# A GNN, mixer and FFN layer: the mixer's products on quarters of the array, its columns laid out so that neighbours are summed, three elementwise steps rewritten, and the FFN weight transposes moved last

## The chip, the cores and the metric

One Trainium2 chip, one of its cores. The time is the device time of one execution in microseconds (us), the median over several runs. The profile is one further execution, recorded by the hardware profiler. The engines are TensorE (PE, with its weight loads shown apart as PEld), VectorE (DVE), ScalarE (ACT), GpSimd (POOL) and SyncE (SP, which here only issues DMAs). Each engine works through its own list of instructions in the order in which they were compiled, and waits at an instruction whose inputs are not there.

## The reference

`x` has 1250 rows of 1024. There are 20000 edges with a source, a destination and one of 8 types.

```python
xn = layernorm(x)
# 1. GNN: per type r the mean over incoming edges, times weight[r]; gate z
u = xn @ root + bias + sum_r mean_r(xn[src]) @ weight[r]
z = concat([u, xn]) @ w_gate + b_gate
gnn = tanh(u) * z + xn * (1 - z)
# 2. mixer: linear attention, 8 heads of 16, features 1, k, k (x) k / sqrt(2)
q, k, v = rms_norm(xn) @ (w_q, w_kv)          # 128 columns each
num = phi(q) @ (phi(k).T @ v);  den = phi(q) @ sum(phi(k))
mix = (num / max(den, 1e-5)) @ w_out
x1 = x + gnn + mix
# 3. FFN with weights and inputs rounded to a 4-bit grid in blocks of 16
h = silu(Q(ln(x1)) @ Q(f_gate).T) * (Q(ln(x1)) @ Q(f_up).T)
out = x1 + Q(h) @ Q(f_down).T                  # 352 hidden columns
```

## The kernel before

Rows are handled in 10 blocks `b` of 128 (the last has 98). The kernel has four stages.

1. Up to about 350 us of the profiled execution: layer norm and transpose of all blocks, the edges sorted by destination, the first products `xn @ weight[r]`.
2. Up to about 1513 us: `product` multiplies `xn` by the other weights, in three products of parts per product (lines 520 to 522). Beside it run the *messages* for each half `nh` of the columns: `gather` (line 435, POOL) fetches 128 rows of `y_d` by an indirect DMA, and `segments` scales them (lines 446 and 448), sums equal destinations by two products with a selection matrix (lines 451 and 452), and stores the sums to `seg_d` (lines 453 and 454). There are 157 messages per half; four buffers `msg` hold gathered rows.
3. The list `rest`, up to about 1687 us. Its pieces are closures that are called in a written order. The loop over them issues, between the pieces, the last messages of the second half, so many per piece that the last one falls before the last `FIRST` = 5 pieces. The order of each engine's instructions is then settled by the compiler's scheduler, near this order.
4. `block(b)`, `hidden`, `finish`: for each block the gate product, the sum `x1`, its layer norm, rounding, and the FFN, software-pipelined over three blocks.

The pieces of stage 3 before the change, in the order of `rest`: four FFN transposes `gate_up` (`ffn_weight`: load a rounded weight tile into `raw`, transpose it on PE, copy it to `wguT`); `mix_sums` (lines 669 and 675); `open_rows` and `open_segments(0)` (segments that cross a tile border: sums of rows of `seg_d` are added to other rows of `seg_d` by indirect DMAs, line 757); four `mix_pair(c)`; eight more `gate_up`; eight `down` (the same transposes, into `wdT`); five `mix_num(b)`. When the last message has been issued, `open_segments(1)` follows. It loads rows of `seg_d` (lines 748 and 749, on SP's queue), multiplies, copies to `osum` and adds to `seg_d`. Only after that may `block` gather its rows `ag` (line 802).

`mix_pair(c)` forms, for two heads and each block, `kk[p, h, i, e] = k[p, h, i] * v[p, h, e]` on DVE (line 686, 512 columns), and a product sums it over the rows with all 128 columns of `k` as the stationary side (line 688). Of the 128 rows of the result only the 32 of the two heads are wanted: line 690 masks the rest to zero when it copies into `bd[:, c, :]`. There are 10 x 4 of these products.

`mix_num(b)` transposes `q` (line 622), and for each of four `c` multiplies it by `bd[:, c, :]` (line 629, 128 rows of contraction of which 96 are zero), multiplies the result by `q` along `i` (`prod`, line 631) and sums over `i` (`num`, line 633). In `prod` the index `i` lies outside `e`, so that the sum runs over elements 16 apart. A further product (lines 635 and 636) gives the linear and constant terms, seven small DVE steps follow (lines 637 to 645), and `mix_transposed` (lines 652 and 653) puts the result into `mixT`. Five of the ten `mix_num` are in `rest`; number 5 comes before the first block and 6 to 9 between later blocks.

In `block(b)` `xn` is made anew from `x` on DVE (line 124), `u` is the sum of the root product and `ag` (line 808), its transpose goes to PE (line 154), ACT takes the tanh (line 811), POOL forms `tanh(u) - xn` and `xn + x` (lines 812 and 813). PE then multiplies by `wg` (line 817) and `wo` (line 820); DVE adds and multiplies (lines 818 to 824). The second normalisation (line 124 again) and `quantize` (lines 133 to 146) are on DVE. `hidden` transposes the result and multiplies by `wguT` (line 841), `finish` by `wdT` (line 857).

Products of stage 3 and 4 write to a pool of four PSUM banks (`mm_tile`), transposes to one of two (`tr_tile`). The pool `wk` of stage 4 lies in memory that the pools of stage 3 gave up, so its first writers wait for the last use of these.

Of the kernel before, what the change touches and what calls it, by code (L numbers as in the profile page):

```python
# [8 lines left out]
F32 = mybir.dt.float32  # L9
# [3 lines left out]
AF = mybir.ActivationFunctionType  # L13
# [12 lines left out]
MORE = 4096  # L26
H, DH = 8, 16
FIRST = 5
LAG = 2
EARLY = 140  # L30
PLAIN = 4
# [11 lines left out]
def rows_of(b):  # L43
    return min(BR, N - b * BR)
# [3 lines left out]
def gps_layer(ctx: ExitStack, tc: tile.TileContext, x, src, dst, et, w_rel, w_root, bias,  # L48
# [24 lines left out]
    def mm_tile():  # L73
        return psum["mm"].tile([128, 512], F32, name="mm")
# [33 lines left out]

    stat = const.tile([BR, NB, 2], F32, name="stat")
    rms = const.tile([BR, NB, 2], F32, name="rms")  # L110
    V.memset(rms, 1.0)
    node_at = const.tile([128, NHI], I32, name="node_at")

# [9 lines left out]
    def normalize(o, xt, mr):  # L123
        V.tensor_scalar(o, xt, mr[:, 0:1], mr[:, 1:2], op0=ALU.subtract, op1=ALU.mult)  # L124
# [488 lines left out]
    bd = mx.tile([128, 4, 512], F32, name="bd")  # L613
# [5 lines left out]
    def mix_num(b):  # L619
        pt = tr_tile()  # L620
        n = rows_of(b)
        T.transpose(pt[:, 0, :n], qn[:n, b, :], ident[:n, :n])
        qT = mx.tile([128, BR], F32, name="qT", bufs=2)[:, :n]
        S.copy(qT, pt[:, 0, :n])
        q3 = h3(qn[:n, b, :])
        num = mx.tile([BR, H, DH], F32, name="num", bufs=2)[:n]
        for c in range(4):
            ps = mm_tile()
            T.matmul(ps[:n], qT, bd[:, c, :], start=True, stop=True)  # L629
            prod = mx.tile([BR, 2, DH, DH], F32, name="prod", bufs=2)[:n]  # L630
            V.tensor_tensor(prod, ps[:n].rearrange("p (h i e) -> p h i e", h=2, i=DH),  # L631
                            q3[:, 2 * c:2 * c + 2, :, None].to_broadcast([n, 2, DH, DH]), ALU.mult)
            V.tensor_reduce(num[:, 2 * c:2 * c + 2], prod.rearrange("p h i e -> p h e i"), AX.X, ALU.add)  # L633
# [12 lines left out]
        nums[b] = num  # L646
# [7 lines left out]

    with ExitStack() as late:
        op = late.enter_context(tc.tile_pool(name="op", bufs=1))
        pb = late.enter_context(tc.tile_pool(name="pb", bufs=2))
        kv = op.tile([BR, NB, 257], F32, name="kv")
        V.memset(kv[:, :, 256:257], 1.0)

# [15 lines left out]
            V.tensor_copy(crow[:, :128], ps[:1, :128])  # L676
            V.memset(crow[:, 128:], float(N))

        def mix_pair(c):
            ps = mm_tile()  # L680
            for b in range(NB):
                n = rows_of(b)
                kk = pb.tile([BR, 2, DH, DH], F32, name="kk")[:n]
                ck = kv[:n, b, c * 32:c * 32 + 32].rearrange("p (h i) -> p h i", h=2)
                cv = kv[:n, b, 128 + c * 32:128 + c * 32 + 32].rearrange("p (h e) -> p h e", h=2)
                V.tensor_tensor(kk, ck[:, :, :, None].to_broadcast([n, 2, DH, DH]),
                                cv[:, :, None, :].to_broadcast([n, 2, DH, DH]), ALU.mult)
                T.matmul(ps, kv[:n, b, :128], kk.rearrange("p h i e -> p (h i e)"),
                         start=(b == 0), stop=(b == NB - 1))
            V.scalar_tensor_tensor(  # L690
                bd[:, c, :].rearrange("p (h x) -> p h x", h=2), ps.rearrange("p (h x) -> p h x", h=2), 0.5,
                mask8[:, 2 * c:2 * c + 2][:, :, None].to_broadcast([128, 2, 256]), op0=ALU.mult, op1=ALU.mult)

# [50 lines left out]
        def open_segments(nh):  # L744
            s1 = op.tile([128, HD], F32, name="s1")
            s2 = op.tile([128, HD], F32, name="s2")
            rows127 = seg_d[nh][:ZERO, :].rearrange("(t p) c -> t p c", p=128)[:, 127, :]
            nc.sync.dma_start(s1, rows127[:128])
            nc.sync.dma_start(s2[:B2], rows127[128:])
            for i, n in enumerate((128, B2)):  # L750
                ps = mm_tile()
                T.matmul(ps[:n], osel[:, 0, i * 128:i * 128 + n], s1, start=True, stop=(i == 0))
                if i == 1:
                    T.matmul(ps[:n], osel[:B2, 1, 128:], s2[:B2], start=False, stop=True)
                osum = op.tile([128, HD], F32, name="osum", bufs=2)
                evac(osum[:n], ps[:n])
                G.indirect_dma_start(
                    out=seg_d[nh][:, :], out_offset=bass.IndirectOffsetOnAxis(ap=orow[:n, i:i + 1], axis=0),
                    in_=osum[:n, :], in_offset=None, compute_op=ALU.add)
# [6 lines left out]
        gate_up = [lambda a=(fgu_d[i * I:(i + 1) * I, :], r0, n, c0, HD, wguT, D_CHUNKS[:4], i * I + r0): ffn_weight(*a)  # L766
                   for i in range(2) for r0, n in I_CHUNKS for c0 in (0, HD)]
        down = [lambda a=(fdn_d, r0, n, 0, I, wdT, I_CHUNKS, r0): ffn_weight(*a) for r0, n in D_CHUNKS]
        rest = gate_up[:4] + [mix_sums, open_rows, lambda: open_segments(0)]
        rest += [lambda c=c: mix_pair(c) for c in range(4)] + gate_up[4:] + down  # L770
        for b in range(FIRST):
            rest.append(lambda b=b: (mix_num(b), mix_transposed(b - 1) if b else None))
        done = EARLY
        for i, p in enumerate(rest):
            p()
            while done < ST + LAG and (done - EARLY) * (len(rest) - FIRST) < (i + 1) * (ST + LAG - EARLY):
                message(1, done)
                done += 1
                if done == ST + LAG:
                    open_segments(1)  # L780
# [6 lines left out]

    turn[0], turns[0] = 1, 0
    wk = ctx.enter_context(tc.tile_pool(name="wk", bufs=1))
    def block(b):  # L790

        rows, n = block_rows(b), rows_of(b)
        xt = ld.tile([BR, D], F32, name="xt")[:n]
        rt = ld.tile([BR, D], F32, name="rt")[:n]
        ag = wk.tile([BR, D], F32, name="ag", bufs=2)[:n]
        gx = ld.tile([BR, D], F32, name="gx")[:n]
        nc.sync.dma_start(xt, x[rows, :])
        nc.sync.dma_start(rt, root_d[rows, :])
        nc.sync.dma_start(gx, gx_d[rows, :])
        with tc.issue_after(gathered_last[0]):  # L800
            for nh, cs in halves:
                G.indirect_dma_start(
                    out=ag[:, cs], out_offset=None, in_=seg_d[nh][:, :],
                    in_offset=bass.IndirectOffsetOnAxis(ap=node_at[:n, b:b + 1], axis=0))
        xn = wk.tile([BR, D], F32, name="xn", bufs=2)[:n]
        normalize(xn, xt, stat[:n, b, :])
        u = wk.tile([BR, D], F32, name="u", bufs=2)[:n]
        V.tensor_tensor(u, rt, ag, ALU.add)
        uT = wk.tile([128, KC, BR], F32, name="uT", bufs=2)
        transpose_cols(uT, u, n, D_CHUNKS, 0)  # L810
        S.activation(u, u, AF.Tanh)
        G.tensor_tensor(u, u, xn, ALU.subtract)
        G.tensor_tensor(xn, xn, xt, ALU.add)
        for nh, cs in halves:
            ps = mm_tile()
            for k in range(KC):
                T.matmul(ps[:n], uT[:, k, :n], wg[:, k, cs], start=(k == 0), stop=(k == KC - 1))  # L817
# [3 lines left out]
            V.tensor_tensor(xn[:, cs], pm[:n], xn[:, cs], ALU.add)  # L821
        V.tensor_tensor(gx, gx, u, ALU.mult)
        x1 = wk.tile([BR, D], F32, name="x1", bufs=3)[:n]
        V.tensor_tensor(x1, xn, gx, ALU.add)

        mr = wk.tile([BR, 2], F32, name="mr", bufs=2)[:n]
        mean_rstd(wk, mr, x1)
# [72 lines left out]
```

## Time and profile before

| | us |
|---|---|
| median of 3 runs | 2048.61 |
| lowest and highest run | 2047.39, 2053.55 |
| the profiled execution, whole | 2055.06 |
| its span from the first to the last instruction | 2053.3 |
| busy in the span: PE, PEld | 1932.2, 1282.5 |
| DVE, ACT, POOL | 1371.5, 719.9, 611.6 |

The span is what the profile's views divide; 1.8 us of the execution lie around it. Busy time of PE counts a product from its start to its modelled end, and products overlap, so that it says little on how well PE is used. In the profile an fp32 product or transpose appears as two records: 40 products of line 629 are 80 records of MATMUL.

### The profile page before, as it was taken

To read this page: it belongs to the slowest core of one execution; us is meant where nothing else is said; L and a number is where in the kernel's file an instruction comes from. 1 tells how busy PE (TensorE), PEld (TensorE's weight loads), DVE (VectorE), ACT (ScalarE), POOL (GpSimd) and SP (SyncE) were. 2 spreads that over 40 slices of the span, in tenths; PEclk is the share of its full clock that TensorE was granted. 3 is DMA by queue.
4 is the path that set the end of the run, shared out by engine and by line. 5 is a ranking of instruction groups with operands and counts; after the bars stand their busy time and mean duration, and the time that the engine had idled before them with its cause. 6 is when DMAs were issued, how large, how long until landed. Compare 5 with 4: busy or idle time off the path is not lost. (4 is left out here: it accounts for less than half of the span.)

```text
span 2053.3 us, 23776 instructions
## 1 busy us (share of the span) xinstructions
PE 1932.2 (94%) x7748; PEld 1282.5 (62%) x7748; DVE 1371.5 (67%) x2944; ACT 719.9 (35%) x1265; POOL 611.6 (30%) x539
## 2 busy tenths in 40 slices
PE   7999999999999999999999989989988879999998
PEld 4465544777777777777777866766753334455544
DVE  8989941677766456545554676665655767988785
ACT  4111241111125545455445455555542211222221
POOL 1000287885013323233323233323332122221110
PEclk9999999999999999999999999999987979999999
DMA  5233222444347776777766688778797422122100
GB/s 205 70 109 123 81 68 63 118 124 125 122 138 234 226 233 215 219 229 229 227 202 220 204 258 255 239 231 255 236 306 259 125 63 82 51 75 75 47 21 29
DMA packets 159346, 327.81 MB, mean 160 GB/s; under 512 B 26414, under 2 KB 35284, under 8 KB 159222
## 3 DMA queue, kind: packets, MB, share of 16 engines
q10 hardware_dynamic: 76570, 141.23, 18.6%
q0 software_dynamic: 33952, 91.27, 17.3%
q1 hardware_dynamic: 48700, 93.79, 14.5%
q8 instruction: 61, 1.00, 0.2%
q14 instruction: 63, 0.52, 0.1%
HBM read 179.54 MB, written 146.49 MB: 159 GB/s over the span
## 5 line engine op out<-in xcount | busy, mean ns | idle before, releaser
L520 PE MATMUL ab<-wH,xH 128*128 128x512 f32 (+3 forms) x1360 | 536.2, 395 | 3.4 <-ACT wH L479 3.2
L522 PE MATMUL ab<-wD,xD 128*128 128x512 f32 (+3 forms) x1360 | 529.9, 395 | 5.8 <-DVE wD L481 4.6
L521 PE MATMUL ab<-wL,xL 128*128 128x512 f32 (+3 forms) x1360 | 532.8, 393 | 0.0
L435 POOL DMA_INDIRECT msg<-y_d,key x314 | 319.5, 1018 | 677.3 <-PE sm L452 388.1
L448 DVE SCALAR_TENSOR_TENSOR msg<-msg,weight,hi 128x512 fp32r<-128x512 f32 x314 | 234.2, 750 | 148.6 <-ACT hi L446 95.1
L522 PEld LDWEIGHTS ab<-wD,xD 128*128 128x128 f32 (+1 forms) x1360 | 253.2, 187 | 77.0 <-DVE wD L481 13.6
L520 PEld LDWEIGHTS ab<-wH,xH 128*128 128x128 f32 (+1 forms) x1360 | 255.3, 188 | 62.1 <-ACT wH L479 5.4
L379 PE MATMUL mm<-wt,xnT 128*128 128x512 f32 (+1 forms) x640 | 292.1, 601 | 0.0
L521 PEld LDWEIGHTS ab<-wL,xL 128*128 128x128 f32 (+1 forms) x1360 | 254.4, 187 | 60.3 <-DVE wL L480 1.1
L361 POOL DMA_INDIRECT sort_d<-pay,row x160 | 202.1, 1263 | 281.7 <-DVE pay L352 233.3
L453 ACT COPY seg<-sm 128x512 f32<-128x512 f32 x314 | 181.6, 584 | 208.4 <-PE sm L452 153.2
L446 ACT ACTIVATE hi<-msg,weight 128x512 fp32r<-128x512 f32 x314 | 221.6, 721 | 89.8 <-DMA msg<-y_d,key 29.7
L529 DVE SCALAR_TENSOR_TENSOR yt<-ab,yt 128x512 f32<-128x512 f32 (+3 forms) x170 | 114.8, 680 | 120.8 <-ACT yt L528 117.0
L528 ACT ACTIVATE yt<-ab 128x512 f32<-128x512 f32 (+3 forms) x170 | 100.0, 592 | 269.2 <-PE ab L521 207.4
L379 PEld LDWEIGHTS mm<-wt,xnT 128*128 128x128 f32 (+1 forms) x640 | 114.6, 188 | 119.7 <-issue 118.7
L444 DVE TENSOR_SCALAR sel<-iota_n,last_row 128x128 fp32r<-128x128 f32 x314 | 89.8, 288 | 111.3 <-PE sm L452 108.5
L451 PE MATMUL sm<-hi,sel 128*128 128x512 f32 x314 | 138.3, 444 | 26.6 <-ACT hi L446 20.6
L452 PE MATMUL sm<-msg,sel 128*128 128x512 f32 x314 | 139.5, 444 | 24.5 <-DVE msg L448 24.3
L817 PE MATMUL mm<-wg,uT 128*128 128x512 f32 (+1 forms) x320 | 141.2, 594 | 1.2 <-ACT uT L87 0.8
L480 DVE TENSOR_TENSOR wL<-raw,h 128x512 fp32r<-128x512 f32 x136 | 93.0, 684 | 69.9 <-PE mm L379 69.9
L479 ACT CAST wH<-h 128x512 fp32r<-128x512 f32 x136 | 83.6, 621 | 132.6 <-DVE h L478 113.5
L817 PEld LDWEIGHTS mm<-wg,uT 128*128 128x128 f32 (+1 forms) x320 | 59.2, 187 | 75.1 <-issue 70.3
(257 smaller groups left out, 2153.9 us busy)
## 6 DMA issues: line engine op xcount, KB each, us to landing
seg_d<-seg ACTq DMA_DIRECT2D x314, 256.0 KB
y_d<-yt ACTq DMA_DIRECT2D x144, 256.0 KB
raw<-in_L_gnn_weight_dram SPq DMA_DIRECT2D x96, 256.0 KB
db<-in_dst_dram SPq DMA_DIRECT2D x32, 312.5 KB
xt<-in_x_dram SPq DMA_DIRECT2D x18, 512.0 KB
wt<-in_L_gnn_weight_dram SPq DMA_DIRECT2D x24, 256.0 KB
msg<-y_d,key POOLq DMA_INDIRECT x314
root_d<-yt ACTq DMA_DIRECT2D x18, 256.0 KB
```

The costliest lines, as they stand in the source:

```text
L361: st = G.indirect_dma_start(out=sort_d[:, :], out_offset=bass.IndirectOffsetOnAxis(ap=row[:, t:t + 1], axis=0), in_=pay[:, t, :], in_offse ...
L379: T.matmul(ps[:n], xnT[:, k, block_rows(b)], held[k], start=(k == 0), stop=(k == KC - 1))
L435: gathered_last[0] = G.indirect_dma_start(out=msg[:, :], out_offset=None, in_=y_d[nh][:, :], in_offset=bass.IndirectOffsetOnAxis(ap=key[:, ...
L446: S.mul(hi, msg, weight[:, t:t + 1])
L448: V.scalar_tensor_tensor(lo, msg, weight[:, t:t + 1], hi.bitcast(F32), op0=ALU.mult, op1=ALU.subtract)
L451: T.matmul(ps, sel, hi, start=True, stop=False)
L452: T.matmul(ps, sel, lo, start=False, stop=True)
L453: S.copy(seg, ps)
L520: T.matmul(pa[:p, :n], xH[:, k, ns], Wh[:, :n], start=(k == 0), stop=False)
L521: T.matmul(pa[:p, :n], xL[:, k, ns], Wl[:, :n], start=False, stop=(k == KC - 1))
L522: T.matmul(pb[:p, :n], xD[:, k, ns], Wd[:, :n], start=(k == 0), stop=(k == KC - 1))
L817: T.matmul(ps[:n], uT[:, k, :n], wg[:, k, cs], start=(k == 0), stop=(k == KC - 1))
```

## The change

- `mix_pair(c)` becomes `mix_pairs(b)`: the four products of one block run on four column quarters of the array (32 columns of `k` each) into four partition quarters of one bank. There is one masked copy into a `bd` of 512 columns for all four. `kk` is laid out as (h, e, i), and has eight buffers in place of two.
- `mix_num`: the four products contract 32 rows each (row quarters of the array), are all issued ahead of the DVE steps, and take all four banks. The sum over `i` runs over neighbouring elements.
- `block`: no `xn` is made. With `r` and `m` the reciprocal deviation and mean of a row, ACT forms `sx = x * (1 + r) - m r` (which is `x + xn`) by a scale and a bias, DVE forms `tanh(u) - r x` and, while it multiplies by the gate, adds `m r`. POOL's two steps are gone. The factors `xf` are made once. The second normalisation is on ACT too, with a bias that one small DVE step makes.
- `rest`: `mix_sums`, `open_rows`, `open_segments(0)`, ten `mix_pairs`, four `gate_up`, five `mix_num`, eight `gate_up`, eight `down`. The messages are spread over all but the last `AFTER` = 8 pieces, which are the `down`.

```diff
-        for c in range(4):
-            ps = mm_tile()
-            T.matmul(ps[:n], qT, bd[:, c, :], start=True, stop=True)
+        pss = [mm_tile() for _ in range(4)]
+        for c, ps in enumerate(pss):
+            T.matmul(ps[:n], qT[32 * c:32 * c + 32], bd[32 * c:32 * c + 32], start=True, stop=True)
+        for c, ps in enumerate(pss):
             prod = mx.tile([BR, 2, DH, DH], F32, name="prod", bufs=2)[:n]
-            V.tensor_tensor(prod, ps[:n].rearrange("p (h i e) -> p h i e", h=2, i=DH),
-                            q3[:, 2 * c:2 * c + 2, :, None].to_broadcast([n, 2, DH, DH]), ALU.mult)
-            V.tensor_reduce(num[:, 2 * c:2 * c + 2], prod.rearrange("p h i e -> p h e i"), AX.X, ALU.add)
+            V.tensor_tensor(prod, ps[:n].rearrange("p (h e i) -> p h e i", h=2, e=DH),
+                            q3[:, 2 * c:2 * c + 2, None, :].to_broadcast([n, 2, DH, DH]), ALU.mult)
+            V.tensor_reduce(num[:, 2 * c:2 * c + 2], prod, AX.X, ALU.add)
...
-        pb = late.enter_context(tc.tile_pool(name="pb", bufs=2))
+        pb = late.enter_context(tc.tile_pool(name="pb", bufs=8))
...
-        def mix_pair(c):
-            ps = mm_tile()
-            for b in range(NB):
-                n = rows_of(b)
+        def mix_pairs(b):
+            if b == 0:
+                bd_ps.append(mm_tile())
+            ps, n = bd_ps[0], rows_of(b)
+            kks = []
+            for c in range(4):
                 kk = pb.tile([BR, 2, DH, DH], F32, name="kk")[:n]
...
-                T.matmul(ps, kv[:n, b, :128], kk.rearrange("p h i e -> p (h i e)"),
+                kks.append(kk.rearrange("p h e i -> p (h e i)"))
+            for c, kk in enumerate(kks):
+                T.matmul(ps[32 * c:32 * c + 32], kv[:n, b, 32 * c:32 * c + 32], kk,
                          start=(b == 0), stop=(b == NB - 1))
...
-        rest = gate_up[:4] + [mix_sums, open_rows, lambda: open_segments(0)]
-        rest += [lambda c=c: mix_pair(c) for c in range(4)] + gate_up[4:] + down
+        rest = [mix_sums, open_rows, lambda: open_segments(0)]
+        rest += [lambda b=b: mix_pairs(b) for b in range(NB)] + gate_up[:4]
         for b in range(FIRST):
             rest.append(lambda b=b: (mix_num(b), mix_transposed(b - 1) if b else None))
+        rest += gate_up[4:] + down
...
-            while done < ST + LAG and (done - EARLY) * (len(rest) - FIRST) < (i + 1) * (ST + LAG - EARLY):
+            while done < ST + LAG and (done - EARLY) * (len(rest) - AFTER) < (i + 1) * (ST + LAG - EARLY):
...
+    xf = wk.tile([BR, NB, 4], F32, name="xf")
+    V.tensor_tensor(xf[:, :, 3], stat[:, :, 0], stat[:, :, 1], ALU.mult)
+    V.tensor_scalar(xf[:, :, 0], stat[:, :, 1], 1.0, None, op0=ALU.add)
+    V.tensor_scalar(xf[:, :, 1], xf[:, :, 3], -1.0, None, op0=ALU.mult)
+    V.tensor_scalar(xf[:, :, 2], stat[:, :, 1], -1.0, None, op0=ALU.mult)
...
-        normalize(xn, xt, stat[:n, b, :])
+        S.activation(sx, xt, AF.Identity, bias=xf[:n, b, 1:2], scale=xf[:n, b, 0:1])
...
-        G.tensor_tensor(u, u, xn, ALU.subtract)
-        G.tensor_tensor(xn, xn, xt, ALU.add)
+        V.scalar_tensor_tensor(u, xt, xf[:n, b, 2:3], u, op0=ALU.mult, op1=ALU.add)
...
-        V.tensor_tensor(gx, gx, u, ALU.mult)
+        V.scalar_tensor_tensor(gx, u, xf[:n, b, 3:4], gx, op0=ALU.add, op1=ALU.mult)
...
+        V.scalar_tensor_tensor(mr[:, 2:3], mr[:, 0:1], -1.0, mr[:, 1:2], op0=ALU.mult, op1=ALU.mult)
...
-        normalize(x2, x1, mr)
+        S.activation(x2, x1, AF.Identity, bias=mr[:, 2:3], scale=mr[:, 1:2])
```

A further memset of `stat` at the start (one DVE instruction) gives the unused rows of the last block a value.

More of the change, by code (lines that the diff above doesn't have):

```diff
@@ L28 @@
 FIRST = 5
+AFTER = 8
 LAG = 2
@@ L110, in gps_layer @@
     rms = const.tile([BR, NB, 2], F32, name="rms")
+    V.memset(stat, 1.0)
     V.memset(rms, 1.0)
@@ L612, in gps_layer @@
     crow = mx.tile([1, 136], F32, name="crow")
-    bd = mx.tile([128, 4, 512], F32, name="bd")
+    bd = mx.tile([128, 512], F32, name="bd")
+    mask2 = mx.tile([128, 2], F32, name="mask2")
+    V.tensor_reduce(mask2, mask8.rearrange("p (c h) -> p h c", h=2), AX.X, ALU.add)
     halves = [(nh, slice(nh * HD, (nh + 1) * HD)) for nh in range(2)]
@@ L677, in mix_sums @@
             V.memset(crow[:, 128:], float(N))
[L679 to L682 removed]
+        bd_ps = []
+        def mix_pairs(b):
[4 more added lines that the diff above has]
+            for c in range(4):
                 kk = pb.tile([BR, 2, DH, DH], F32, name="kk")[:n]
@@ L685, in mix_pair @@
                 cv = kv[:n, b, 128 + c * 32:128 + c * 32 + 32].rearrange("p (h e) -> p h e", h=2)
-                V.tensor_tensor(kk, ck[:, :, :, None].to_broadcast([n, 2, DH, DH]),
-                                cv[:, :, None, :].to_broadcast([n, 2, DH, DH]), ALU.mult)
-                T.matmul(ps, kv[:n, b, :128], kk.rearrange("p h i e -> p (h i e)"),
+                V.tensor_tensor(kk, ck[:, :, None, :].to_broadcast([n, 2, DH, DH]),
+                                cv[:, :, :, None].to_broadcast([n, 2, DH, DH]), ALU.mult)
+                kks.append(kk.rearrange("p h e i -> p (h e i)"))
+            for c, kk in enumerate(kks):
+                T.matmul(ps[32 * c:32 * c + 32], kv[:n, b, 32 * c:32 * c + 32], kk,
                          start=(b == 0), stop=(b == NB - 1))
-            V.scalar_tensor_tensor(
-                bd[:, c, :].rearrange("p (h x) -> p h x", h=2), ps.rearrange("p (h x) -> p h x", h=2), 0.5,
-                mask8[:, 2 * c:2 * c + 2][:, :, None].to_broadcast([128, 2, 256]), op0=ALU.mult, op1=ALU.mult)
+            if b == NB - 1:
+                V.scalar_tensor_tensor(
+                    bd.rearrange("p (h x) -> p h x", h=2), ps.rearrange("p (h x) -> p h x", h=2), 0.5,
+                    mask2[:, :, None].to_broadcast([128, 2, 256]), op0=ALU.mult, op1=ALU.mult)
         B2 = ST - 128
@@ L804, in block @@
                     in_offset=bass.IndirectOffsetOnAxis(ap=node_at[:n, b:b + 1], axis=0))
-        xn = wk.tile([BR, D], F32, name="xn", bufs=2)[:n]
-        normalize(xn, xt, stat[:n, b, :])
+        sx = wk.tile([BR, D], F32, name="sx", bufs=2)[:n]
+        S.activation(sx, xt, AF.Identity, bias=xf[:n, b, 1:2], scale=xf[:n, b, 0:1])
         u = wk.tile([BR, D], F32, name="u", bufs=2)[:n]
@@ L820, in block @@
             T.matmul(pm[:n], mixT[:, rows], wo[:, cs], start=True, stop=True)
-            V.tensor_tensor(xn[:, cs], pm[:n], xn[:, cs], ALU.add)
-        V.tensor_tensor(gx, gx, u, ALU.mult)
+            V.tensor_tensor(sx[:, cs], pm[:n], sx[:, cs], ALU.add)
+        V.scalar_tensor_tensor(gx, u, xf[:n, b, 3:4], gx, op0=ALU.add, op1=ALU.mult)
         x1 = wk.tile([BR, D], F32, name="x1", bufs=3)[:n]
-        V.tensor_tensor(x1, xn, gx, ALU.add)
-        mr = wk.tile([BR, 2], F32, name="mr", bufs=2)[:n]
-        mean_rstd(wk, mr, x1)
+        V.tensor_tensor(x1, sx, gx, ALU.add)
+        mr = wk.tile([BR, 3], F32, name="mr", bufs=2)[:n]
+        mean_rstd(wk, mr[:, :2], x1)
+        V.scalar_tensor_tensor(mr[:, 2:3], mr[:, 0:1], -1.0, mr[:, 1:2], op0=ALU.mult, op1=ALU.mult)
         x2 = wk.tile([BR, D], F32, name="x2", bufs=2)[:n]
-        normalize(x2, x1, mr)
+        S.activation(x2, x1, AF.Identity, bias=mr[:, 2:3], scale=mr[:, 1:2])
         quantize(wk, x2, x2, n, D, bufs=1)
```

## The prediction

> **What bounds the kernel now.** I read the chain of waits first. It can be followed back only to 1642.8 us and holds 411 us of the 2053.3: PE with the gate, FFN and mixer products, and at its beginning a stretch of DVE. So I cut the end of the span into stages with the view of busy time by stretch (columns: length, then busy time and count of PE, PEld, DVE, ACT, POOL, then granted clock, DMA share, GB/s):
>
> ```profile
> 1513.00:1560.00 47.00, 35.08 (x116) 20.42 (x116) 24.31 (x71) 19.82 (x34) 13.77 (x14) 0.67 1.02 366
> 1560.00:1611.00 51.00, 45.13 (x117) 19.46 (x116) 35.63 (x60) 9.98 (x17) 11.55 (x9) 0.93 0.48 152
> 1611.00:1629.00 18.00, 11.59 (x45) 7.05 (x44) 7.57 (x19) 9.96 (x22) 2.85 (x3) 0.81 0.60 202
> 1629.00:1643.00 14.00, 11.08 (x29) 3.87 (x27) 13.18 (x23) 0.93 (x4) 1.62 (x1) 1.00 0.21 43
> 1643.00:1653.00 10.00, 4.54 (x6) 1.70 (x6) 0.00 (x0) 0.01 (x1) 2.12 (x1) 0.68 0.07 8
> 1653.00:1687.00 34.00, 25.36 (x49) 10.55 (x49) 32.47 (x64) 1.50 (x6) 7.69 (x8) 0.69 0.30 93
> 1730.00:1860.00 130.00, 127.03 (x385) 67.02 (x383) 110.45 (x174) 31.70 (x51) 26.95 (x14) 0.98 0.21 69
> ```
>
> The first is DMA-bound (share 1.02, clock 0.67). The second is the 40 products of `mix_pair`: PE leads, DVE is 70% busy. The third waits for FFN weight loads. The fourth and the sixth are six `mix_num`, where DVE is 94 to 95% busy. The fifth is a hole. From 1730 us on PE is the bound (127 of 130 us). The hole is the tail of the last message, in POOL's and DVE's timelines (start, length, instruction, idle before):
>
> ```profile
> 1637.07 1.62 POOL L757 DMA_INDIRECT seg_d<-osum,orow  x1 [22.57 <-DMA s<-seg_d]
> 1643.93 2.12 POOL L757 DMA_INDIRECT seg_d<-osum,orow  x1 [5.24 <-issue]
> 1653.97 1.03 POOL L802 DMA_INDIRECT ag<-seg_d,node_at  x1 [7.93 <-issue]
> 1653.30 0.81 DVE L124 TENSOR_SCALAR xn<-xt,stat 128x1024 f32<-128x1024 f32 x1 [10.54 <-issue]
> ```
>
> Two adds to `seg_d` follow each other, and the first gather `ag` follows the second. DVE stands at `xn` for 10.54 us because `wk` lies in memory that these DMAs still hold. Behind `xn` are four `mix_num`, 34 us of DVE, and behind these in PE's list the first transposes of `u` (1687.3) and the first gate product (1688.6). So before, the tail of the messages and the mixer's DVE work lie one after the other. The prices of the mixer's steps, by tile:
>
> ```profile
> L688 PE MATMUL mm<-kk,kv x80: 590/592/1219, 1559.6 to 1609.4; 128*128 128x512 f32 x72, 98*128 98x512 f32 x8
> L686 DVE TENSOR_TENSOR kk<-kv x40: 681/691/694, 1520.8 to 1608.2; 128x512 f32<-128x512 f32 x36, 98x512 f32<-98x512 f32 x4
> L629 PE MATMUL mm<-bd,qT x80: 590/592/1222, 1628.5 to 1823.3; 128*128 128x512 f32 x72, 128*98 128x512 f32 x8
> L633 DVE TENSOR_REDUCE num<-prod x40: 915/1006/1035, 1630.2 to 1829.4; 128x32 f32<-128x512 f32 x36, 98x32 f32<-98x512 f32 x4
> L133 DVE TENSOR_REDUCE q_sc<-hs x10: 505/520/521, 1759.7 to 2036.1; 128x22 f32<-128x352 f32 x9, 98x22 f32<-98x352 f32 x1
> L133 DVE TENSOR_REDUCE q_sc<-x x10: 1206/1220/1221, 1717.9 to 2013.7; 128x64 f32<-128x1024 f32 x9, 98x64 f32<-98x1024 f32 x1
> ```
>
> **The change part by part.** *Quarter products.* A product is two records, 0.43 us apart in the timeline of PE, so the four of a `mix_num` take 3.43 us and the 40 of `mix_pair` 34. No row here shows products on quarters. The Trainium skill, page "TensorE: Matmul & The Clock Gate", section "Part 3: Packing small matmuls", has four row quarters of 512 columns run 3.07 times faster, and says that matmuls start and end in program order. By the first, four products take 1.1 us. But both records of an fp32 product sit on one quarter, and in program order only the second of one product can run beside the first of the next: five slots of 0.43 for eight, 2.14 us (an estimate from the row's pitch and that rule). Ends: 1.1 and 3.5 (no overlap). I take 2.14.
>
> *Sum over neighbours.* The strided sum of 512 takes 1006 ns. Contiguous rows of 352 and 1024 take 520 and 1220, so by the line through both 512 takes 0.69; back to back 0.61 for 0.92. Ends: 0.31 us saved in each of 40, or nothing. I take the saving: a `mix_num` costs DVE 4 x 0.60 + 4 x 0.61 + 1.2 for its small steps = 6.0 us, for 7.3. A rule speaks against the quarter products here: "TensorEngine Tiling (Array Packing)", section "Performance Considerations", warns that a faster array leaves the PSUM copy as bottleneck. The stage rows agree (DVE 95%, PE 75%): in `mix_num` I count the DVE time alone, 6.0 us each; by the products' speed alone it would be 3.4 - 2.1 = 1.3 us more each.
>
> *First stretch, 1513 to 1560.* The compiled order shows that five messages instead of eight, and three FFN tiles instead of seven, now lie ahead of `open_segments(0)`, and that `wo`, `xt` and `rt` queue on SP behind the second load of line 748, which waits for that step. It moved 366 GB/s x 47 us = 17.2 MB; 3 x 0.5 + 4 x 0.25 + about 1 MB fall away, 3.5 MB or 9.5 us. Left: 38 us, until 1551.
>
> *`mix_pairs`.* Eight of 40 `kk` are made in the first stretch (eight buffers; DVE was 52% busy there). DVE then has 32 x 0.61 + seven messages x 0.95 + 1.2 = 27.4 us, PE 10 x 2.14 + 7 x 0.46 = 25. I take 30, until 1581, for 51. POOL's second add of `open_segments(0)` holds the gathers behind it for about 9 us, as before (8.84); five messages have been gathered by then, and PE comes to the sixth only after 24 `kk`.
>
> *Five `mix_num` before the end of the messages.* 5 x 6.0 + six messages x 0.95 + one copy = 36.4 of DVE; I take 38, until 1619. PE waits for a bank at each `mix_num`, since four are taken at once; behind it in the list are only messages, which are prepared four deep.
>
> *Eight `gate_up` with the last five messages.* Eight tiles at the about 1.3 us that loads with three buffers allow, and five messages: 12 us. The last line 452 then runs at 1631; before it ran at 1628.1. So the messages end no sooner, but the mixer's work is done.
>
> *From the last message to the gate product.* Before, 25.9 us lie from line 452 to the gather. Eight `fdn_d` loads now stand before line 749's load on SP while `down` runs: +1.5. Then the second gather (2.3), its landing (4), line 808 (1.2). On ACT the copies of `uT` come behind two `sx` of 1.1 us, and these behind `mixT`, which waits for `mix_num(5)`: 3.4. 1631 + 1.5 + 25.9 + 2.3 + 4 + 1.2 + 3.4 = 1669.3, for 1688.6: -19.3. The `down` tiles (about 10 us) and `mix_num(5)` (6 us) lie inside the 25.9; if the tail were shorter than them they would show.
>
> *Blocks.* PE-bound, so four `mix_num` could save 1.3 us each in products. But the banks of its third and fourth product are free only after line 845 or 858 on DVE, and line 635 waits for the first `prod`, which comes one long step earlier in DVE's new order. Number 6 gives nothing (PE waits 2.6 us for DVE's rounding of block 0 anyway), 7 about 1.0, 8 and 9 about 1.5: -4. The rewritten sums move work: DVE loses two steps of 0.80 and gains one of 1.22 and one of 0.16; ACT gains two of about 1.1 each; POOL loses two of 2.3. None of it is on the path while PE is the bound. The one new wait: on ACT the second normalisation stands behind the silu of the block before, and the copies `hT`, which PE's line 857 awaits, behind both. In the block at 1908 the square root can run at 1914.3, the silu at 1915.8, the normalisation until 1917.4; `hT` was due at 1920.0. Cover 2.7 us; beyond it each us costs a us. Six of 28 table loads (1.28 us) go, off the path.
>
> The start's memset of `stat` is under 0.1 us beside the first loads. Sum: -19.3 - 4 = -23.3, on the profiled execution 2055.1 - 23.3 = 2031.8. That execution lies 6.5 us above the median; from the median 2048.6 I get 2025.
>
> **Rivals.** *The DVE floor.* If the five messages never stall DVE, stretch one ends at 1545, the two mixer stages take 27.4 and 36.4 and the transposes 8: last message at 1617, -33; with products at 1.1 us two more in the blocks: 2009. For it: DVE idles 61 of 174 us now. Against: gathers wait up to 7.3 us under load.
>
> *The quarters don't overlap.* PE then bounds `mix_pairs` with 34 + 3 + switching, 41 for 30, and the blocks give nothing: -23 + 11 + 4 = -8, 2040. For it: no row shows overlap, and the tiling page has a change of mode drain PE; messages on the full array cut in between the groups. Against: even then the other work of the change fills the hole.
>
> *Slower: the messages end later.* The last 17 messages now stand in PE's list behind all mixer products. If PE, at the clock of 0.69 that the `mix_num` stage shows, and DVE take turns instead of overlapping, because all four banks are held, a `mix_num` takes 10.5 us (PE 4.5, DVE 6.0) and `mix_pairs` 41: the last message at 1631 + 22 + 11 = 1664, the gate product at 1702, +13.7; the blocks no better: 2062. It decides from 1654 on for the last line 452.
>
> *The blocks lose it.* If `hT` is 1 us late in each of ten blocks, and with it PE: -13, 2035.
>
> **How the numbers follow.** Main case 0.52 (2025), DVE floor 0.14 (2009), no overlap 0.17 (2040), slower 0.11 (2062), blocks 0.06 (2035). 0.3%, 6 us, is about what a measurement of this kernel can tell from no change. Slower by more: the third rival, 0.11. Within: a third of the no-overlap case and the edge of the main one, 0.09. Faster: 0.80. Range 2006 to 2047: the floor case and no overlap with its bounds, leaving out the slower rival and a little of the floor.
>
> **What would show it.** Right: the hole at 1643 gone, first gate product (line 817 before) near 1669, last message near 1631, the sum over neighbours at 0.69 us, `mix_pairs` about 30 us long with DVE above 80% busy, and blocks as long as before less 4 us. Quarter products that start beside each other, 0.43 us apart at most in pairs, show the order argument; four starting at once, the 3.07. Wrong: a last message after 1654, or PE idle at line 857 for `hT` in every block.

## The result and the profile after

The changed kernel takes 2031.6 us (median of 6 runs, 2025.4 to 2034.5), the kernel before beside it 2048.4. The ratio is 0.9919, with a 95% interval of 0.9902 to 0.9936: faster by 0.8%. The profiled executions are 2055.1 and 2034.5 us, 20.6 us apart.

Not all of these 20.6 us are due to the change. The load of `kv`, which opens the changed part, starts at 1513.1 us before and at 1508.9 after; over the runs below it starts between 1501.5 and 1513.1. So stages are counted from that load from here on. From it to the first gate product it is 175.5 us before and 162.1 after (1671.0 - 1508.9), from there to the end of the span 364.7 and 361.7. That is -13.4 and -3.0, together -16.4, which agrees with the -16.8 of the medians.

The stages of the changed kernel, as the table of windows gives them. The columns are window, length, busy time of PE, PEld, DVE, ACT and POOL with instruction counts, granted clock, DMA share, GB/s:

```profile
1513.00:1545.00 32.00, 25.77 (x92) 15.18 (x96) 18.99 (x51) 12.67 (x22) 10.17 (x10) 0.69 1.04 389
1545.00:1574.00 29.00, 26.76 (x100) 6.98 (x100) 25.00 (x44) 7.71 (x14) 17.18 (x8) 0.94 0.80 261
1574.00:1621.00 47.00, 45.07 (x82) 15.22 (x80) 35.16 (x84) 8.82 (x18) 5.70 (x6) 0.50 0.23 73
1621.00:1636.00 15.00, 9.47 (x51) 6.29 (x49) 7.33 (x19) 6.77 (x13) 1.35 (x1) 0.84 0.63 196
1636.00:1653.00 17.00, 12.77 (x36) 5.58 (x35) 5.77 (x13) 4.20 (x11) 1.80 (x2) 0.50 0.38 95
1653.00:1662.00 9.00, 0.00 (x0) 0.00 (x0) 0.00 (x0) 0.00 (x0) 1.94 (x1) 0.50 0.07 7
1662.00:1671.00 9.00, 1.78 (x8) 1.57 (x8) 4.87 (x15) 2.96 (x3) 4.85 (x5) 0.50 0.50 137
```

The rows are: first stretch; `mix_pairs`; five `mix_num`; eight `gate_up` with the last messages; `down`; the hole; gathers, `u` and its transposes. The DMA-bound stretch is shorter (36 us from the load of `kv`, of which the first row shows the last 32, for 47), and `mix_pairs` takes 29 us where `mix_pair` took 51. But the third row is the longest stage: PE's records fill 45 of 47 us at a granted clock of 0.50, and DVE, which bounded `mix_num` before, is only 75% busy. The hole is there as before. It now stands in front of `xf` instead of `xn`, as the timelines of POOL and DVE show (start, length, instruction, idle time before it):

```profile
1645.84 1.61 POOL L769 DMA_INDIRECT seg_d<-osum,orow  x1 [20.17 <-issue]
1652.82 2.12 POOL L769 DMA_INDIRECT seg_d<-osum,orow  x1 [5.36 <-ACT mixT L658]
1662.27 0.18 DVE L805 TENSOR_TENSOR xf<-stat 128x10 f32<-128x10 f32 x1 [9.75 <-issue]
1662.96 1.03 POOL L822 DMA_INDIRECT ag<-seg_d,node_at  x1 [8.02 <-DVE xf L807]
```

Two of the mixer steps shown before, by tile (line, engine, shortest/median/longest ns, first and last start):

```profile
L699 PE MATMUL mm<-kk,kv x80: 592/617/1063, 1544.9 to 1572.3; 128*32 128x512 f32 x72, 98*32 98x512 f32 x8
L638 DVE TENSOR_REDUCE num<-prod x40: 626/676/687, 1580.8 to 1805.7; 128x32 f32<-128x512 f32 x36, 98x32 f32<-98x512 f32 x4
```

The sum over neighbours went from 1006 to 676 ns. A single record of a product is no shorter than before; what is new is that records run beside each other, which the timeline of PE shows and this row doesn't. At full clock (first fence: `mix_pairs`, then two `mix_num` of the blocks) four products (x8, two records each) take 1.07 us on column quarters and 1.27 on row quarters, and one takes 1.12. The first row is the same group as the second, seen through a window of 0.04 us: the first records of all four products start in it. The four second records follow about 0.45 us later. In the stage of the five `mix_num`, at half clock (second fence), one product takes 2.07 us and two take 2.08:

```profile
1544.90 0.64 PE L699 MATMUL mm<-kk,kv 128*32 128x512 f32 x4
1544.90 1.07 PE L699 MATMUL mm<-kk,kv 128*32 128x512 f32 x8
...
1689.57 1.12 PE L633 MATMUL mm<-bd,qT 32*128 32x512 f32 x2 [0.25 <-DVE sx L840]
1720.99 1.27 PE L633 MATMUL mm<-bd,qT 32*128 32x512 f32 x8 [0.25 <-ACT qT L628]
```

```profile
1578.04 2.07 PE L633 MATMUL mm<-bd,qT 32*128 32x512 f32 x2
1580.04 0.80 PE L454 MATMUL sm<-msg,sel 128*128 128x512 f32 x1
1580.76 2.08 PE L633 MATMUL mm<-bd,qT 32*128 32x512 f32 x4
```

So quarters on different strips cost little more than one product, not four, as long as they follow each other. A message product between them, as at 1580.04, splits the group, and each piece pays the full 2.07 us. DVE's waits in that stage say the same:

```profile
DVE prod L636 <- PE mm L633: 11.5, 7, 2.9
```

### The profile page after: what moved, and what is told of

Same layout as the page of the kernel before. It is cut to its first block, busy times and chain, and to the rows that moved or that the text cites. A ratio compares the mean times of both kernels' runs of the same rounds, so it can differ in the third digit from the quotient of the medians.

```text
span 2032.7 us, 23764 instructions
## 1 busy us (share of the span) xinstructions
PE 1916.1 (94%) x7748; PEld 1266.7 (62%) x7748; DVE 1319.7 (65%) x2947; ACT 736.0 (36%) x1279; POOL 569.5 (28%) x519
## 5 line engine op out<-in xcount | busy, mean ns | idle before, releaser
L437 POOL DMA_INDIRECT msg<-y_d,key x314 | 327.5, 1043 | 682.8 <-PE sm L454 402.1
```

Of the source, the lines that this page charges most:

```text
L437: gathered_last[0] = G.indirect_dma_start(out=msg[:, :], out_offset=None, in_=y_d[nh][:, :], in_offset=bass.IndirectOffsetOnAxis(ap=key[:, ...
```

## The experiments

The theory on record was that the new order carries the gain, because the mixer's work then lies ahead of the tail of the messages. The rivals that the runs tell apart: the shorter pair products, the contiguous sum, the rewritten sums of the block, or the quarters in `mix_num`. The columns on the right come from each run's profiled execution: from the load of `kv` to the last message's product (line 454 in the changed kernel), to the first gate product, and from there to the end of the span. The kernel changed was profiled twice, and its two values of the second column, 162.1 and 167.7, show how far one execution can be trusted: about 6 us. The runs were made in three groups, each with the kernel before beside it (medians 2046.8, 2045.3 and 2046.2 us), so across groups the ratios compare better than the medians.

| kernel | median us | ratio to before, 95% | last message | gate product | gate to end |
|---|---|---|---|---|---|
| before | 2048.4 | | 115.0 | 175.5 | 364.7 |
| changed | 2031.6 | 0.9919 [0.9902, 0.9936] | 126.9 | 162.1 | 361.7 |
| changed, again | 2033.7 | 0.9929 [0.9910, 0.9948] | 131.8 | 167.7 | 361.9 |
| order undone | 2025.1 | 0.9888 [0.9856, 0.9920] | 94.1 | 151.0 | 361.5 |
| order alone | 2050.0 | 1.0010 [0.9994, 1.0026] | 134.2 | 173.1 | 363.7 |
| block undone | 2035.2 | 0.9939 [0.9915, 0.9962] | 121.4 | 157.8 | 359.7 |
| AFTER = 16 | 2030.3 | 0.9914 [0.9885, 0.9942] | 109.3 | 157.5 | 358.6 |
| whole array in `mix_num` | 2024.1 | 0.9903 [0.9884, 0.9922] | 115.5 | 150.5 | 364.1 |
| strided sum | 2036.3 | 0.9948 [0.9930, 0.9967] | 129.9 | 165.7 | 362.4 |
| `xf` ahead, AFTER = 16 | 2021.8 | 0.9890 [0.9866, 0.9915] | 113.6 | 158.2 | 358.8 |
| order undone, whole array in `mix_num` | 2021.5 | 0.9891 [0.9869, 0.9912] | 95.0 | 151.6 | 363.1 |
| whole array in `mix_pairs` | 2047.6 | 1.0001 [0.9986, 1.0017] | 143.2 | 179.2 | 361.8 |
| hybrid, AFTER = 12 | 2023.6 | 0.9889 [0.9867, 0.9911] | 114.0 | 153.2 | 361.3 |
| hybrid, old order | 2010.4 | 0.9813 [0.9787, 0.9839] | 95.7 | 140.0 | 361.8 |

### The order, undone and alone

```diff
-        rest = [mix_sums, open_rows, lambda: open_segments(0)]
-        rest += [lambda b=b: mix_pairs(b) for b in range(NB)] + gate_up[:4]
+        rest = gate_up[:4] + [mix_sums, open_rows, lambda: open_segments(0)]
+        rest += [lambda b=b: mix_pairs(b) for b in range(NB)] + gate_up[4:] + down
         for b in range(FIRST):
             rest.append(lambda b=b: (mix_num(b), mix_transposed(b - 1) if b else None))
-        rest += gate_up[4:] + down
...
-            ... (done - EARLY) * (len(rest) - AFTER) ...
+            ... (done - EARLY) * (len(rest) - FIRST) ...
```

> The changed kernel with the old order of the list (four gate_up, sums, open_segments(0), mix_pairs, eight gate_up, down, then the five mix_num) and the old spread of messages; quarter products, layout and blocks stay. Theory A (the shorter mixer carries the gain, the new order little): open_segments(0) done at 1560 as before, mix_pairs 28 us, gate_up and down 18, last message at 1606, hole, four mix_num of 6 to 7 us, first gate product at 1660 to 1668: 2022 to 2030 us. Theory B (the order carries it, because mix_num must not stand behind the adds' tail): first gate product later than 1680, 2038 us or more.

Measured: 2025.1 us, first gate product at 1660.3, the last message at 1603.4. Theory A's numbers. Without the new order the kernel isn't slower; by the ratios it is 6 to 8 us faster than the changed kernel, though the intervals overlap a little. It has the order of the kernel before, and up to the last message it differs from it in `mix_pairs` alone, with its buffers and its ten pieces in the list; the last message comes 20.9 us earlier (115.0 - 94.1). The opposite run applies the new order and spread to the kernel before, with `mix_pair(c)` in the place of `mix_pairs(b)` and nothing else (the diff above, reversed):

> The kernel before with only the new order of the list and the new spread of messages; whole-array products in four banks, strided sums and blocks as before. Theory A: first stretch 15 us shorter, mix_pair 51 us, five mix_num of 7.3 with six messages 43 us, gate_up 15, tail 27: first gate product at 1681, 2041 us (-7). Theory B (the order carries the gain): 2034 us or less. If the order gains nothing by itself: 2048.

Measured: 2050.0 us, ratio 1.0010, the third expectation. The order alone gives nothing. It did what it says: from the last message to the gate product it is 38.9 us (173.1 - 134.2) instead of 60.5. But the last message comes 19.2 us later, because the mixer's work now lies ahead of it. The order moves this work from one side of the last message to the other, and the hole stays. So the theory on record falls, for the new order as the carrier. The hole in the run with the order undone:

```profile
1628.34 0.18 DVE L804 TENSOR_TENSOR xf<-stat 128x10 f32<-128x10 f32 x1 [8.03 <-issue]
```

DVE stands 8.03 us at `xf`, though most of four `mix_num` wait behind it. Both orders lose this time.

### The block's sums

```diff
-        sx = wk.tile([BR, D], F32, name="sx", bufs=2)[:n]
-        S.activation(sx, xt, AF.Identity, bias=xf[:n, b, 1:2], scale=xf[:n, b, 0:1])
+        xn = wk.tile([BR, D], F32, name="xn", bufs=2)[:n]
+        normalize(xn, xt, stat[:n, b, :])
...
-        V.scalar_tensor_tensor(u, xt, xf[:n, b, 2:3], u, op0=ALU.mult, op1=ALU.add)
+        G.tensor_tensor(u, u, xn, ALU.subtract)
+        G.tensor_tensor(xn, xn, xt, ALU.add)
...
```

> The changed kernel with the block's sums as before (xn by DVE, two POOL steps, x2 by DVE). Prediction's working (off the path while PE is the bound): 2030 to 2034 us, first gate product to end of span 361 to 364 us as in the changed kernel. If the rewritten sums carry a part: 2036 us or more.

Measured: 2035.2 us, between the two expectations, with an interval that overlaps both intervals of the changed kernel, and 359.7 us from gate product to end, no longer than with the rewritten sums. The traced execution is the fastest of its seven (2023.2 us). It shows no gain from the rewritten sums; the medians, 1.5 to 3.6 us apart, leave room for a small one and can't say more.

### The messages' end

```diff
-AFTER = 8
+AFTER = 16
```

> The changed kernel with AFTER = 16 for 8: the messages end before the last eight gate_up, so that these and down lie in the tail of the adds. Theory A (the tail of the last message, 27 us, is the path, and 9.7 us of it are a hole): last message at about 1622, hole gone, first gate product at 1662 to 1664, 2023 to 2026 us. Theory B (the messages then press on mix_num, which grows by what the tail gains, or the gathers are too late): 2030 to 2034 us.

Measured: 2030.3 us, theory B's time, and the hole isn't gone. The last message comes 17.6 us earlier, but 48.2 us lie between it and the gate product (157.5 - 109.3) instead of 35.2. The timelines of DVE and PE:

```profile
1640.72 0.18 DVE L805 TENSOR_TENSOR xf<-stat 128x10 f32<-128x10 f32 x1 [9.53 <-DMA seg_d<-osum,orow]
1641.37 0.90 PE L156 MATMUL tr<-ident,raw 128*128 128x128 f32 x3 [9.22 <-DVE wdT L90]
```

Now the copies of `down` stand behind `xf` on DVE, and PE's transposes behind these copies, so that the work that was to cover the tail can't run in it. The next version computes `xf` ahead of the mixer:

```diff
-AFTER = 8
+AFTER = 16
...
-    xf = wk.tile([BR, NB, 4], F32, name="xf")
+    xf = const.tile([BR, NB, 4], F32, name="xf")
...
-        sx = wk.tile([BR, D], F32, name="sx", bufs=2)[:n]
+        sx = ld.tile([BR, D], F32, name="sx")[:n]
```

> The changed kernel with AFTER = 16, xf computed once ahead of the mixer in memory of its own, and sx in the pool of xt, so that no DVE or ACT step stands in the adds' tail for wk's memory. Theory A (the 9.5 us of DVE idleness at xf keep the copies of down, and with them PE, behind the tail): copies of down done by the time that ag lands, first gate product some 8 us earlier than with AFTER = 16 alone, 2020 to 2023 us. If down's loads or PE's clock bound the tail: 2028 to 2031.

The median, 2021.8 us, is within what theory A gave, but the trace doesn't show its mechanism: the gate product comes at 158.2 us, not earlier than with AFTER = 16 alone, and the intervals of the two runs overlap. The wait at `xf` is gone, and another has taken its place, `u` waiting for `ag` ahead of the copies of `down`:

```profile
1652.65 1.23 DVE L827 TENSOR_TENSOR u<-rt,ag 128x1024 f32<-128x1024 f32 x1 [11.09 <-DMA ag<-seg_d,node_at]
```

### Quarters or the whole array in `mix_num`

```diff
-    bd = mx.tile([128, 512], F32, name="bd")
+    bd = mx.tile([128, 4, 512], F32, name="bd")
+    V.memset(bd, 0.0)
...
-            T.matmul(ps[:n], qT[32 * c:32 * c + 32], bd[32 * c:32 * c + 32], start=True, stop=True)
+            T.matmul(ps[:n], qT, bd[:, c, :], start=True, stop=True)
```

The mask step of `mix_pairs` writes the four strips of `bd` in four steps.

> The changed kernel with whole-array products in mix_num alone (bd again four tiles with zeros outside the pair's 32 rows, filled from the one bank of mix_pairs in four steps); mix_pairs keeps its quarters. Theory C (quarter products let the granted clock fall to half, and at half the group of four costs 2.07 us and is PE's bound in the stage): clock over 0.9 in the stage of the five mix_num, the stage 38 to 40 us instead of 46.5, 2024 to 2027 us. Theory D (the clock falls because the stage asks little of PE, whatever the products' shape): clock 0.5 to 0.6, stage 52 us or more, 2037 us or more. If the products' time doesn't matter there: 2032.

Measured: 2024.1 us. Windows of this run (the first `mix_pairs`, the second the five `mix_num`), and two rows from PE's timeline:

```profile
1541.00:1569.00 28.00, 27.83 (x102) 7.56 (x94) 27.08 (x48) 8.66 (x16) 19.02 (x8) 1.00 0.80 264
1569.00:1604.00 35.00, 30.32 (x84) 13.26 (x83) 34.05 (x82) 8.05 (x19) 4.70 (x5) 0.95 0.29 90
```

```profile
1587.60 3.70 PE L634 MATMUL mm<-bd,qT 128*128 128x512 f32 x8 [0.41 <-ACT qT L629]
1591.50 0.71 PE L641 MATMUL mm<-rl,qT 128*128 128x264 f32 x2 [0.20 <-DVE prod L637]
```

Theory C's numbers. With products that take 3.70 us for four instead of 1.07, the stage is shorter: 36 us from its first product (1566.75) to its last transpose (1603.1), where it is 47 in both traces of the changed kernel (1574.5 to 1621.9 in the first). The clock stays at 0.95. DVE, 97% busy in the window, is the bound again, as the prediction had taken it to be for the quarters, and PE is the one that waits (0.20 us for `prod` in the second row). In the blocks the quarters are worth something: 364.1 us from gate product to end with the whole array, for 361.7. By the ratios the kernel is 3 to 5 us faster than the changed one, and the intervals overlap. So that quarters in `mix_num` are a loss on the whole isn't shown. That they lengthen this stage is: the hybrid with AFTER = 12, below, has whole-array products in it as well, and it takes 35 us at a clock of 1.00. A lowered clock goes with it, at which one product takes 2.07 us for 1.12; no run has quarters in this stage at full clock, so that the clock makes the difference is argued from these times. What lowers the clock stays open: in the changed kernel it fell about 4 us ahead of the first product of the stage (0.81 from 1565 to 1574, 0.50 from there on), with AFTER = 16 about 6 us after it, and in neither did it rise again before the stage was nearly over.

With the old order the same edit was to give 6 us:

> Old order of the list (as in the run with the order undone, 2025 us) with whole-array products in mix_num. Theory C: the four mix_num behind the hole take 6.0 to 6.5 us instead of 8.0, clock 0.9 or more there, first gate product 6 us earlier, 2018 to 2021 us. Theory D (the clock falls in the hole and stays down): each of the four takes 9 us or more, 2028 us or more.

Measured: 2021.5 us and a gate product at 151.6, for 151.0 with quarters. The time is 0.5 us outside theory C's range. From `xf` to the gate product, with four `mix_num`, it is 30.9 us for 32.0 with quarters, and DVE stands 11.65 us at `xf` for 8.03. The clock was 0.79 in the hole (1608 to 1624, PE busy for 5.77 us of 16) and 0.71 behind it:

```profile
1624.00:1654.00 30.00, 24.98 (x55) 11.27 (x56) 26.41 (x66) 4.14 (x9) 7.69 (x8) 0.71 0.34 105
```

Neither theory holds here. After a stretch in which PE had little to do, whole-array products ran at a lowered clock as well, but it did not stay down as in the run with quarters (0.50).

### The strided sum

```diff
-            V.tensor_reduce(num[:, 2 * c:2 * c + 2], prod, AX.X, ALU.add)
+            V.tensor_reduce(num[:, 2 * c:2 * c + 2], prod.rearrange("p h i e -> p h e i"), AX.X, ALU.add)
```

`kk`, `bd` and `prod` are laid out (h, i, e) to match.

> The changed kernel with kk, bd and prod laid out (h, i, e) as before, so that the sum over neighbours is strided again (1.0 us for 0.69); all else as changed. If DVE bounds mix_num, as the prediction took it: five times 1.3 us before the messages' end and part of the sixth, 2038 us or more. If PE at half clock bounds it (theory C): 0 to 2 us, 2031 to 2034.

Measured: 2036.3 us, between the two expectations. By the ratios it is 4 to 6 us slower than the changed kernel; the intervals overlap a little.

```profile
1574.00:1624.00 50.00, 45.17 (x82) 14.86 (x80) 41.96 (x84) 9.57 (x20) 6.91 (x8) 0.53 0.25 79
```

The stage of five `mix_num` takes 50 us for 47. DVE works 6.8 us more in it (41.96 - 35.16) and 2 to 3 us of that show. So at half clock PE and DVE share the bound: neither is it alone.

### Whole-array products in `mix_pairs`

```diff
-        def mix_pairs(b):
+        def mix_pair(c):
+            ps = mm_tile()
+            for b in range(NB):
...
-                T.matmul(ps[32 * c:32 * c + 32], kv[:n, b, 32 * c:32 * c + 32], kk,
+                T.matmul(ps, kv[:n, b, :128], kk.rearrange("p h e i -> p (h e i)"),
                          start=(b == 0), stop=(b == NB - 1))
```

> The changed kernel with whole-array products in mix_pairs alone (pair by pair as before, four banks one after the other, contiguous layout kept); mix_num keeps its quarters, order and blocks stay. Theory A (the shorter pair products carry most of the gain): the stage takes 48 to 52 us instead of 28, first gate product 18 to 23 us later, 2046 to 2054 us. If the gain came from elsewhere (order, sum, blocks): 2036 to 2041 us.

Measured: 2047.6 us, ratio 1.0001: the whole gain is gone. Its window of the pair products:

```profile
1550.00:1586.00 36.00, 36.00 (x89) 16.54 (x88) 26.71 (x43) 3.80 (x7) 5.51 (x4) 1.00 0.47 159
```

The time is as theory A gave it, the stage is not: 36 us, PE-bound, not 48 to 52. Of the 16.3 us by which the last message is later than in the changed kernel (143.2 - 126.9), about 7 are the stage itself (36 for 29), 3 lie ahead of it and 6 behind it. With four pieces instead of ten in the list, only four messages fall into the stage, for seven in the changed kernel, and 14 come after it, for 11. This run doesn't part the quarters from this spread of the messages.

It also keeps the eight buffers of `kk`, and these are a rival that no run takes away alone. With two buffers PE had to wait for `kk`, 5.87 us in one place in the kernel before (first row) and 9.08 us in the run with the order alone (second row). In this run it nowhere stands idle for `kk`:

```profile
1582.92 3.78 PE L688 MATMUL mm<-kk,kv 128*128 128x512 f32 x4 [5.87 <-DVE kk L686]
1571.26 2.07 PE L689 MATMUL mm<-kk,kv 128*128 128x512 f32 x2 [9.08 <-DVE kk L687]
```

The stage of whole-array products takes 51 us in the first, with eight messages, and 59 in the second, with ten; here it takes 36, with four. So a part of the 22 us between `mix_pair` and `mix_pairs` belongs to the buffers and to the work that stands elsewhere now, and about 7 to the quarters. What is shown is that `mix_pairs` as a whole carries the gain, and that without the quarters in it none is left in this order, where `mix_num` runs at half clock.

### The changed kernel again, and two combinations

> The changed kernel itself, beside the others on this chip: 2026 to 2033 us, ratio to before 0.990 to 0.993; load of kv to first gate product 162 us, as in its first trace.

Measured: 2033.7 us, 0.7 above the expected range; the ratio, 0.9929, lies within it. The load of `kv` to the gate product took 167.7 us in this execution, not 162.

Both combinations use the whole array in the first five `mix_num`, quarters in the five of the blocks, and `xf` and `sx` as above:

```diff
+            if b < FIRST:
+                T.matmul(ps[:n], qT, bd[:, c, :], start=True, stop=True)
+            else:
+                T.matmul(ps[:n], qT[qs], bd[qs, c, :], start=True, stop=True)
```

> The changed kernel with whole-array products in the first five mix_num and quarters in the five of the blocks, AFTER = 12, xf computed ahead of the mixer and sx in the pool of xt. Theories A and C together: last message 16 us earlier than in the changed kernel, tail of 27 to 30 us covered by four gate_up and down, first gate product 18 to 22 us earlier, blocks as in the changed kernel: 2010 to 2016 us. If the loads of raw or PE's clock in the tail bound it: 2018 to 2024 us.

Measured: 2023.6 us with AFTER = 12 in the new order. The time is the second expectation's. The last message is 13 us earlier, but the gate product follows 39 us after it. The stage of the five `mix_num` runs at full clock:

```profile
1582.00:1618.00 36.00, 31.49 (x86) 13.81 (x87) 35.84 (x85) 9.90 (x20) 6.29 (x7) 1.00 0.31 102
```

In the tail of the adds DVE now stands 8.88 us at `u`. The first add comes 13.3 us after the last message (1637.6 - 1624.3), for 10.0 in the changed kernel, and on SP's queue the load for it stands behind four `fdn_d` loads. That accounts for some 3 of the 39 us.

The other has the old order, and ties `u` behind the fifth `mix_num` on DVE:

```diff
+        with tc.issue_after(num_last[0]):
             V.tensor_tensor(u, rt, ag, ALU.add)
```

> Old order of the list with whole-array products in the first five mix_num and quarters in the five of the blocks, xf computed ahead, sx in the pool of xt, and the sum u of the blocks kept behind the fifth mix_num on DVE. If the idle time of the tail in the old order came from what waits for wk's memory and for ag: mix_num fills it, first gate product 12 to 18 us earlier than with the old order alone (133 to 139 us after the load of kv instead of 151), 2008 to 2014 us. If DVE and PE still stand in the tail: 2018 us or more.

Measured: 2010.4 us, ratio 0.9813, the fastest of all; its interval lies clear of every other. The gate product comes at 140.0 us, 1 us after the expected range, the time within it. In the tail of the adds, where DVE stood idle for 8 to 12 us in the other kernels, it now works (first row: the run with only the order undone; then this run):

```profile
1613.00:1630.00 17.00, 9.45 (x20) 3.11 (x20) 8.24 (x24) 1.24 (x3) 3.65 (x3) 0.50 0.17 20
1614.00:1632.00 18.00, 15.11 (x38) 6.35 (x36) 15.93 (x40) 0.87 (x4) 4.60 (x3) 0.91 0.16 19
1632.00:1650.00 18.00, 14.28 (x38) 7.09 (x39) 16.37 (x38) 1.88 (x7) 4.57 (x6) 0.73 0.27 79
```

DVE is busy 88% of the time between 1614 and 1632, where it was busy for 8.24 us of 17 in the other, and PE's clock is 0.91 there, for 0.50. Against the run with the old order and whole-array products (gate product at 151.6 us) the gain ahead of the gate product is that of `xf`, `sx` and `u`, apart from the sixth `mix_num`; these were moved together, and no run parts them. This filled tail is what the prediction expected of the change, reached by other means: not by moving `mix_num` ahead of the messages' end, but by leaving it behind and taking away what stood in front of it.

## Why the prediction was right, and where it was not

The sign and the range came true; the working did so only in part. The sum gave -23.3 us. Measured from the load of `kv` it is -16.4. Part of the success is luck: the path that the text named for the gain, the hole filled by the new order, gave nothing, and it is the kernel with the old order that takes the 2025 us predicted for the new one.

- **First stretch.** Right. 38 us were predicted, 36.1 passed from the load to `osum` (1545.0 - 1508.9).
- **Quarter products.** Wrong: 2.14 us for four, measured 1.07. The argument took it that the two records of one product start ahead of the next product's. In the trace the first records of all four start together and the second ones behind them, which is the sign that the text itself had named for the higher figure. The figure of the Trainium skill, page "TensorE: Matmul & The Clock Gate", section "Part 3: Packing small matmuls", 3.07 times, was near: from first start to last end, 3.70 / 1.07 = 3.5 on column quarters and 3.70 / 1.27 = 2.9 on row quarters. The error cost nothing in `mix_pairs`, since DVE bounds it (25.0 us of 29, and PE's next `kk` comes from it).
- **Sum over neighbours.** Right: 0.69 us predicted, 0.68 measured.
- **`mix_pairs`.** Right: 30 us predicted, 28.4 measured from the copy of `osum` to the last mask step, and of all parts this one carries the gain, with the eight buffers in it.
- **Five `mix_num` ahead of the messages' end.** This is the term that was mis-sized: 38 us, measured 47. It counted DVE alone, 6.0 us for each, and put the products' time at nothing beside it. The granted clock fell to 0.50, the quarters took 2.07 us, and messages split the groups. DVE then waited 11.5 us for PE. Only the slower rival had a clock in it.
- **Last message.** 118 us after the load of `kv` (1631 - 1513), measured 126.9: 9 us by the term above and 3 by the eight `gate_up` (15 for 12), less 1.9 and 1.6 in the first two stages, which makes 8.5 of the 8.9.
- **Tail.** 38.3 us from last message to gate product, measured 35.2. Right in size, but "the hole gone" failed: DVE idles 9.75 us as before, only with less work behind it.
- **What the order is worth.** The text put the hole first and let the mixer's new place account for the gain. The two runs on the order show that its place is worth nothing. The mixer's work of stage 3 was 51 + 5 x 7.3 = 87.5 us and is 29 + 47 = 76 now, which is 11.5 of the 13.4 us gained ahead of the gate product; `mix_pairs` saved 22 and `mix_num` gave 10.5 back. The sum came out near because it added stage lengths, and most of these held; those of the mixer would have been gained in the old order too.
- **Blocks.** -4 predicted, -3.0 measured. From gate product to end it is 363.1 to 364.7 us in the four runs with whole-array products in the blocks' `mix_num`, and 358.6 to 362.4 in the ten with quarters, which puts the gain with the quarters, as the text had it. Its remark on the banks holds as well: at 1758.1 three products start together and the fourth 0.85 us later, when line 878 (858 before) has emptied its bank. The rewritten sums give nothing that shows.

Of the rivals, the DVE floor didn't come, since DVE waited for PE. "The quarters don't overlap" is refuted by the 1.07 us. The slower rival named PE's clock, and PE and DVE taking turns, as the mechanism. The clock fell further than it assumed, and DVE waited for PE, but for 11.5 us of 47 only, so a `mix_num` took 9.4 us, not 10.5, and `mix_pairs` was not touched, so that the last message stayed well short of 1654. "The blocks lose it" did not come: PE's waits for `hT` in the blocks are what they were, 2.5 us in six places, here in the changed kernel:

```profile
PE mm L877 <- ACT hT L88: 2.5, 6, 0.5
```

## What to carry to other kernels

A hole in the trace is filled by what can run in it, not by moving work to the other side: look at which instruction stands at it, on each engine, and why (here small steps whose memory the transfers still held, then a sum placed too early in DVE's list). An order that moves work from behind a wait to ahead of it makes the wait begin later by about as much. Packing products onto parts of the array pays where PE is the bound; where another engine is, check the granted clock of the stage afterwards: here the packed stage ran at half clock and took 11 us longer than the same stage unpacked.

## What the runs showed of the hardware

Four fp32 products on column quarters take 1.07 us together, four on row quarters 1.27, a single one 1.12, all of 512 columns at full clock, where four on the whole array take 3.70.

The granted clock fell to 0.50 in a stage where PE's records cover 45 of 47 us, and stayed at 0.95 in the same place with whole-array products of the same results, which cover 30 of 35. It was 0.50 to 0.62 from the first product to the last transpose of this stage in all seven traces of the new order with quarters there, and 0.95 to 1.00 in the three with the whole array. The same page of the Trainium skill, "Part 1: The HAM clock gate", has the clock halved when the array has been idle and raised by sustained work. By PE's records the stage with the lower clock is the busier one, so busy time in the records is not what decides; the runs don't show whether it is the part of the array in use, or the time that the same work would take at full clock. Quarters do not always lower it: `mix_pairs` ran at 1.00 on column quarters in the run with whole-array products in `mix_num`, and in the blocks, between whole-array products, row quarters ran at full clock.
